# A new order of work, with one copy and half of a load given to ScalarE and five filler transposes taken out

## The chip, the cores and the metric

The kernel runs on one core of a Trainium2 chip. The metric is the device time of one execution in microseconds (us), lower is better. TensorE (PE) multiplies, VectorE (DVE), ScalarE (ACT) and GpSimd (POOL) do the elementwise work, and SyncE (SP) issues most of the transfers between the chip's memory and the on-chip memory. Each engine takes its own instructions strictly in the order in which they were written, and waits where a tile that it needs is not ready.

## The reference, cut to what matters

One transformer block over 16 batches (B) of 256 rows (S) of 256 features (E), all in float32:

```
a  = attention(x; 16 heads of 16, one key mask for all batches) @ Wo.T
a  = rms_norm(a) * (1 + gain(cond)) + shift(cond)        # per batch
kx, vx, rx = three mixes of a with a shifted by one row
k, v, r    = kx @ ak.T, vx @ av.T, rx @ ar.T
y  = sigmoid(r) * wkv(k, v)          # a decaying sum along the rows: two scans and a division
x1 = x + y @ ao.T
z  = fixed quaternion rotation of x1
g, u = fp4(z) @ fp4(w_gate).T, fp4(z) @ fp4(w_up).T       # 704 hidden features
out  = x1 + fp4(silu(g) * u) @ fp4(w_down).T
```

`fp4` rounds each block of 16 numbers to a 4-bit grid scaled by the block's maximum. The products above, 16 times, are nearly all of TensorE's work.

## The kernel before, in words

All work is cut into stages, each written as a Python generator that emits some instructions and yields. A stage has one letter and, for most, a batch number in hexadecimal: `a` (ask: load the next x, turn x, make q, k, v), `t` (attend), `l` (leave: Wo and the norm), `m` (mix: the recurrence), `r` (rotate), `h` and `i` (the hidden layer of the two row halves), `d` and `e` (turning its result), `f` (the down product and the output). The setup has stages too: `L` (loads), `Q`, `O`, `A` (turning the weights of the attention and the recurrence), `K` (mask and small vectors), `M` (gain and shift), `T`, `R` (decay and rotation), `W0` to `W5` and `V0`, `V1` (quantizing and turning the weights of the hidden layer) and `C` (a check at the end).

The string `ORDER`, 1884 tokens long, is the whole schedule: a loop takes its tokens one by one and resumes the named stage once. What a resumed stage emits is appended to the instruction stream of each engine in that order, so the string fixes the order on TensorE, VectorE, ScalarE, GpSimd and on SP's queue alike. Work that is emitted ahead of the loop (fillers of zero, the first activation, the first products on zeros) is merged in by the framework.

The string `BANKS` has one digit for each use of the eight PSUM banks, in the order of allocation. A product that is given a bank waits for the last reader of what was there before. A score group of `t` (lines 763 and 771) takes four banks at once, and the exponentials that empty them (L781) run on ScalarE, one for each bank. For batches 0 and 1, called whole, q and k are copied once by ScalarE (L726 and L737); later batches take a way through memory (`parts`, `spread`).

The opening: `load_x(0)` (L165) issues x of batch 0 in four transfers of 32 partitions each; Wq is issued by ScalarE's queue (L237), Wk and Wv by SP (L243). `turn_w` (from L325) turns each with four transposes into a bank (L334); after those of Wq, TensorE also transposes a tile of zeros eight times into a bank that nobody reads (L338). VectorE copies the turned Wq, Wk, Wv and Wo out of their banks (L342), ScalarE the four matrices of the recurrence (L344). VectorE turns x (L670), and the products of q and k (L632) and v (L644) follow. The fourth yield of `loads` issues ten small vectors from ScalarE's queue (L255 and L257), whose transpose is L350. x has two buffers, so the load of batch b + 2 waits until x of batch b has been turned.

Of the kernel before, what the change touches and what calls it, by code (L numbers as in the profile page):

```python
# [28 lines left out]
L af L Q L W1 a0 Q L Q a0 Q V0 a0 a1 a0 a0 a1 L W1 a0 W5 Q V0 L Q W1 a1 a1 a1 t0 a1 t0 K t0 W1 K W4 a0 t1 L W5 L  # L29
t1 a2 L t1 a2 W5 K W1 t0 W4 K W0 W4 K t0 R V0 a2 a3 M K A a3 a0 t0 L a1 W4 W5 a1 a2 M t0 K A t1 R t1 L t0 t0 t1  # L30
t0 W2 R O t0 t1 t0 W5 M T O W2 t1 t0 t0 a2 t1 V0 t0 a4 t1 L t1 t1 t0 t1 W3 t0 M t0 a2 W4 t1 W1 a2 t1 R V0 A l0
a2 R l0 a2 M W0 l0 V0 W0 W3 l0 W5 M A t1 W3 A t1 l0 W2 t1 T a3 R l0 l0 a2 m0 l0 a3 l1 A l1 W0 m0 m0 R W1 m0 m0
m0 m0 m0 a2 l1 a2 m0 l1 t2 W5 V0 R t2 t2 t2 a3 m0 V1 m0 m0 t2 t2 m0 W3 l1 t2 W3 m0 l1 m0 t2 t2 t2 t2 R t2 t2 t2
R m0 V0 t2 W0 W0 l1 m1 a3 W4 a3 a3 m0 V0 W3 l1 t2 m1 W3 a3 t2 t2 W2 W2 W0 A m1 m1 l2 A m1 m1 W4 l2 r0 m1 l2 m1
l2 r0 a4 a3 m1 m1 l2 l2 m1 m1 l2 m2 m1 m1 l2 m1 a3 m2 t3 a3 t3 m2 t3 t3 t3 m1 a4 t3 r0 r0 t3 r0 t3 a4 t3 t3 t3
m2 a4 t3 t3 a5 m2 W2 a4 V1 m2 t3 a4 t3 r0 t3 m2 m1 r0 t3 r0 a4 r1 m2 m2 a4 r1 t3 r1 r0 a4 W2 a5 a4 l3 l3 a6 m2
l3 V1 r1 m2 r0 a5 i0 a5 m2 i0 r1 r1 m2 i0 l3 V1 a4 t4 r1 m2 t4 t4 h0 i0 V1 t4 t4 i0 V1 m2 a5 t4 i0 h0 i0 h0 h0
t4 t4 i0 V1 t4 t4 t4 t4 i0 t4 a5 l3 t4 a5 r1 l3 r1 t4 m2 m2 h0 l3 a5 m3 l3 m3 t4 V1 a5 m3 i0 i0 a5 r2 r1 t4 h0
t4 m3 m3 r2 i0 m3 h0 a5 m3 l4 l4 a6 m3 l4 m3 m3 i0 a6 a5 l4 m3 m3 V1 a6 m3 t5 m3 t5 i1 i0 m3 t5 t5 i0 m3 t5 t5
e0 h0 i1 i1 e0 a6 t5 i1 t5 t5 t5 t5 h0 t5 t5 m3 i1 l4 t5 r2 a6 r2 t5 r2 l4 a7 t5 l4 i1 i1 d0 h0 i1 a6 h0 m4 r3  # L40
l4 m4 m4 h0 a6 a6 t5 d0 h1 m4 h0 r3 r2 i1 t5 h1 h1 a6 a6 i1 h1 m4 m4 h0 a7 r2 h1 i0 i1 h0 a6 h1 m4 a7 m4 a7 i1
m4 t6 h1 e0 t6 m4 m4 e0 t6 m4 l5 t6 i1 l5 t6 t6 r2 h0 d0 l5 m4 i1 h1 i1 t6 r2 m4 a7 m4 t6 d0 t6 l5 l5 t6 t6 r3
t6 t6 r3 t6 l5 a7 r2 e1 l5 r3 m4 a7 t6 d1 r3 i2 a7 r3 a7 f0 i1 i2 h2 i2 r3 i2 r3 f0 m5 l5 h2 e1 m4 a7 m5 a8 i2
h2 m5 h2 a7 i2 i2 h2 h1 r4 h2 h1 a7 h2 h1 d1 f0 h1 t7 i2 f0 t6 t7 f0 r4 t7 t7 h1 e1 t7 h1 m5 t7 t6 e1 t7 m5 h1
a8 t6 t7 m5 t7 t7 t7 a8 r4 h1 m5 t7 h2 d1 a8 r4 t7 d1 m5 r4 a8 a8 d2 l6 t7 m5 l6 l6 l6 i2 m5 i2 i2 r4 r3 m5 a8
i2 m5 r4 a8 l6 m5 h2 t7 a8 m5 h2 i2 h2 a8 m5 f1 l6 i2 m5 i2 i3 a9 a8 h2 h2 l6 i3 f0 f1 i3 h2 f1 i3 a8 l6 h2 m6
h2 d2 m6 m6 t8 f1 t8 t8 t7 t8 e2 i2 f1 i3 m5 t8 d2 r5 i3 i3 d2 r5 t7 a9 t7 t8 t8 t8 e2 t8 i3 e2 t8 a9 t8 a9 t8
t8 e3 m6 l7 m6 t8 l7 m6 t8 a9 r4 h3 h3 l7 l7 a9 r4 m6 m6 a9 l7 h3 e2 m6 a9 h3 l7 h3 a9 m6 m6 h3 f2 l7 i3 a9 i3
m6 i3 m6 h3 f2 i3 l7 m7 h3 m6 i3 i3 m6 m6 a9 aa m7 h3 i3 h3 h3 f1 h3 f2 m7 a9 e3 t9 t8 t9 t9 t9 f2 m6 r4 d3 f2
i3 t9 r6 h3 h3 t9 d3 e3 t8 h3 r6 t8 t9 h3 aa t9 t9 d3 e3 r5 r5 t9 r5 aa i4 i4 t9 l8 d3 t9 i4 m7 i4 aa i4 ab r5  # L50
h4 l8 i4 r5 m7 l8 h4 i4 f2 l8 aa t9 h4 h4 aa t9 m7 r5 h4 h4 l8 l8 i4 m7 h4 l8 t9 m7 m7 aa aa h4 m7 m7 i4 m7 m7
d4 m8 i4 i4 f3 aa aa l8 m7 m8 h4 m7 i4 i4 f3 m7 h4 m7 i4 m8 aa d4 r7 f3 h4 aa h4 i4 h4 ta f3 ta ta t9 f3 ta r7
ab h4 ac h4 ta e4 r7 t9 ab r7 e4 ta ab i4 ta r7 h4 r5 t9 ta ta r7 m8 ta ta ta ta r7 d4 r5 r6 ab r6 ta m8 m8 e4
m8 ab ab ta r6 m8 m8 m8 m8 l9 ab r6 h5 l9 m8 i5 h5 r6 i5 d4 m8 ab h5 l9 i5 h5 ab i5 e4 h5 i5 h5 h5 h5 ab l9 i5
m8 m8 r6 h5 h5 h5 tb h5 tb ta tb i5 tb m8 m8 r6 ab h5 l9 f4 tb l9 tb tb h5 i5 h5 tb e5 f4 ta ta e5 tb h5 tb tb
tb l9 f4 d5 r8 f4 f4 l9 tb r8 d5 r6 d5 ac m9 f4 tb r7 r8 r7 la tb la h6 h6 la r8 r8 h6 i5 i5 h6 m9 la d5 h6 la
i5 r7 i5 m9 m9 la ac m9 r8 m9 i5 m9 m9 ac i5 m9 la m9 ma m9 ac i6 m9 i7 m9 ac r8 h6 r8 ac m9 i5 i5 m9 i6 i6 ac
e5 m9 ac i7 h6 ac la i7 h6 ma e5 i6 f5 i7 f5 i6 i7 ma i6 i7 m9 f5 ad i6 f5 d6 h7 r9 h6 i6 i7 h6 h6 h6 ac f5 h7
h7 ac d6 tc tc r9 h6 tb h6 h7 tc ad tc ad ae h7 tc tc h6 tb h7 tc ad h7 tc tc tb r9 tc ad tc tc i7 ma h7 tc r9
h6 d6 ad i6 r9 ma tc e6 ma ad tc i6 i6 ma i6 h7 r9 r9 i7 f5 ma i6 r8 ma ad e6 r8 i6 lb ad h7 i7 h7 i6 h8 ma i6  # L60
i7 ma ad i7 ma e6 ma h7 h8 d6 i7 lb ad r9 e6 i7 h8 ma h7 ma r9 lb h7 i7 h8 td lb tc h7 ad td h8 td td td ma h8
lb h8 td e7 lb lb f6 lb f6 e7 mb td f6 i7 mb tc mb h8 ma tc h7 td td d7 f6 ra d7 i8 td f6 td i8 td ra r9 td e7
ae i8 i8 td d7 ra i8 mb i8 e7 f6 ra i8 i9 ae d7 i9 mb ra mb i9 i9 lc ra mb ae mb td h8 mb lc ae h8 i9 lc i8 i9
lc ra ae i9 lc mb h8 ae lc h8 mb h9 lc ra h8 mc ae h8 h9 h9 ra ae mb h9 ae h8 mb mb td d8 lc i8 h9 i8 mb h9 mc
# [1197 lines left out]
```

## Time and profile before

| What | us |
|---|---|
| median of 3 runs | 645.22 (645.11 to 645.31) |
| profiled execution, its own time | 645.53 |
| span of its instructions | 643.7 |
| TensorE busy | 635.6 (99%) |
| VectorE busy | 579.0 (90%) |
| ScalarE busy | 391.2 (61%) |
| GpSimd busy | 161.4 (25%) |

A line of the timeline has the start in us from the first instruction, the duration, the engine, the source line, the operation, the tiles (out<-in), the form and how many instructions are merged into it; what is in brackets is the idle time of the engine ahead of it and who ended it. PEld is TensorE's loading of weights, which overlaps the products. SPq and ACTq are the issuing of transfers by SP and ScalarE. A line of the waits names who waited for whom, with the total in us, the number of times and the longest. The end of a matmul is modelled, so its busy time can hide a wait; the distance from one start to the next does not. The granted clock of TensorE was 1.00 over the span.

| stretch of the span, us | PE busy | DVE busy | ACT busy |
|---|---|---|---|
| 0 to 40 | 38.86 | 34.16 | 25.98 |
| 40 to 200 | 159.65 | 142.37 | 116.41 |
| 200 to 400 | 199.95 | 178.77 | 125.40 |
| 400 to 600 | 199.49 | 190.51 | 107.51 |
| 600 to 643 | 37.67 | 33.14 | 15.88 |

### The profile page before, as it was taken

The page shows a single profiled execution, that of the slowest core. Times are in us where ns is not written, and L with a number is a line of the kernel's source. Part 1 is how long each engine was busy: PE and PEld are TensorE (multiplying, and loading weights), DVE is VectorE, ACT ScalarE, POOL GpSimd, SP SyncE. Part 2 cuts the span into 40 slices and gives each one's busy share as a digit, 9 for nine tenths or more (in the row PEclk, how much of TensorE's full clock was granted, in tenths as well). Part 3 has the DMA queues.
Part 4 walks back from the last instruction along what each step waited for, and adds up shares of the span by engine and source line. Part 5 has one row for each costly group of instructions (what it writes and reads, how often), then busy time and mean ns, then how long its engine had stood idle before and what let it go on. Part 6 is the DMA issues. An engine that isn't in the chain of part 4 may idle for free.

```text
span 643.7 us, 11304 instructions
## 1 busy us (share of the span) xinstructions
PE 635.6 (99%) x3936; PEld 475.9 (74%) x3936; DVE 579.0 (90%) x1178; ACT 391.2 (61%) x903; POOL 161.4 (25%) x214
## 2 busy tenths in 40 slices
PE   9999999999999999999999999999999999999996
PEld 7568877677777778777777777777877778776675
DVE  7897899889898877999998999999999999999994
ACT  3879784776757577674766546666483755433332
POOL 3353213222231122131221313113130122112220
PEclk9999999999999999999999999999999999999999
DMA  6643525334251425333420334203204100001001
GB/s 169 172 149 120 167 87 174 99 99 133 82 166 35 154 57 166 78 100 116 148 67 18 126 102 149 67 17 131 82 34 151 47 2 16 1 1 35 0 26 46
DMA packets 62848, 57.72 MB, mean 90 GB/s; under 512 B 36912, under 2 KB 40896, under 8 KB 62784
## 3 DMA queue, kind: packets, MB, share of 16 engines
q1 hardware_dynamic: 62416, 56.65, 29.4%
q8 instruction: 33, 0.54, 0.4%
q10 hardware_dynamic: 368, 0.28, 0.1%
q14 instruction: 31, 0.25, 0.1%
HBM read 38.03 MB, written 18.87 MB: 88 GB/s over the span
## 4 chain that ended last, share of the span: by engine, by line
PE 83%; DVE 12%; issue 2%; ACT 1%; DVEq 0%; ACTq 0%
PE ps L632 24%; PE ps L1003 18%; PE ps L793 9%; PE ps L644 8%; PE ps L1072 7%; PE pss L771 5%; PE ps L608 3%; PE ps L965 2%; PE pss L763 2%; DVE v L562 1%; DVE ps L554 1%; PE ps L656 1%; DVE ps L561 1%; DVE ps L1019 1%; PE ps L1079 1%
## 5 line engine op out<-in xcount | busy, mean ns | idle before, releaser
L1003 PE MATMUL ps<-guT,xqT 128*128 128x320 f32 (+1 forms) x512 | 165.6, 461 | 0.6 <-DVE v L562 0.6
L781 ACT ACTIVATE w<-pss 128x512 f32<-128x512 f32 x256 | 133.6, 609 | 32.7 <-PE pss L771 28.8
L1003 PEld LDWEIGHTS ps<-guT,xqT 128*128 128x128 f32 x512 | 94.7, 190 | 42.0 <-DVE v L562 1.7
L564 POOL TENSOR_TENSOR hq<-v,am 128x320 f32<-128x320 f32 (+1 forms) x64 | 50.0, 787 | 175.8 <-DVE v L562 154.4
L698 POOL TENSOR_TENSOR two<-two 128x512 f32<-128x512 f32 x28 | 35.7, 1275 | 114.2 <-ACT two L691 79.1
L793 PE MATMUL ps<-w,v_one 128*32 128x256 f32 x1024 | 63.1, 382 | 0.1
L559 ACT ACTIVATE m<-ps 128x384 bf16<-128x384 f32 (+1 forms) x64 | 29.8, 467 | 53.2 <-DVE ps L557 52.9
L1072 PE MATMUL ps<-hT,downT 128*128 128x256 f32 x260 | 59.6, 379 | 0.0
L1072 PEld LDWEIGHTS ps<-hT,downT 128*128 128x128 f32 x260 | 48.8, 190 | 8.1 <-ACT w L781 0.3
L936 DVE RECIPROCAL den<-den 128x512 f32<-128x512 f32 x16 | 53.5, 3343 | 0.1
L793 PEld LDWEIGHTS ps<-w,v_one 128*32 128x32 f32 x1024 | 31.8, 109 | 25.3 <-ACT w L781 3.6
L1015 ACT ACTIVATE th<-ps 128x320 f32<-128x320 f32 (+1 forms) x64 | 29.8, 469 | 26.9 <-PE ps L1003 26.1
L771 PEld LDWEIGHTS pss<-qT,kT 64*128 64x128 f32 x448 | 31.0, 185 | 19.3 <-issue 8.9
L771 PE MATMUL pss<-qT,kT 64*128 64x256 f32 x448 | 42.6, 306 | 0.1
L561 DVE SCALAR_TENSOR_TENSOR ps<-m,ps 128x384 f32<-128x384 bf16 (+1 forms) x64 | 33.2, 518 | 6.0 <-ACT m L559 5.8
L562 DVE SCALAR_TENSOR_TENSOR v<-m,ps 128x384 f32<-128x384 bf16 (+1 forms) x64 | 33.3, 521 | 4.9
L557 DVE SCALAR_TENSOR_TENSOR ps<-ps,rs 128x320 f32<-128x320 f32 (+1 forms) x64 | 34.1, 533 | 2.2
L554 DVE TENSOR_REDUCE ps<-ps 128x20 f32<-128x320 f32 (+1 forms) x64 | 34.1, 532 | 2.2
L608 PE MATMUL ps<-ident,hq 128*128 128x128 f32 (+1 forms) x204 | 34.5, 283 | 0.4 <-POOL hq L564 0.2
L1019 DVE SCALAR_TENSOR_TENSOR ps<-th,ps 128x320 f32<-128x320 f32 (+1 forms) x64 | 33.2, 518 | 1.1 <-PE ps L1003 0.4
L1017 DVE SCALAR_TENSOR_TENSOR th<-th,ps 128x320 f32<-128x320 f32 (+1 forms) x64 | 32.1, 507 | 0.4 <-ACT th L1015 0.3
L608 PEld LDWEIGHTS ps<-ident,hq 128*128 128x128 f32 (+1 forms) x204 | 22.0, 136 | 13.1 <-issue 4.0
(200 smaller groups left out, 1288.2 us busy)
## 6 DMA issues: line engine op xcount, KB each, us to landing
kept<-two SPq DMA_DIRECT2D x28, 512.0 KB, 3.2
qT<-kept SPq DMA_DIRECT2D x112, 128.0 KB, 2.9
kT<-kept SPq DMA_DIRECT2D x112, 128.0 KB, 2.8
x_sb<-in_x_dram SPq DMA_DIRECT2D x64, 64.0 KB, 2.3
out_dram<-o_sb SPq DMA_DIRECT2D x52, 64.0 KB, 1.9
out_dram<-o_sb SPq DMA_DIRECT2D x6, 128.0 KB, 2.3
raw<-in_L_ffn_w_down_dram SPq DMA_DIRECT2D x2, 352.0 KB, 3.9
raw<-in_L_ffn_w_gate_dram SPq DMA_DIRECT2D x5, 128.0 KB, 3.3
```

Of the source, the lines that this page charges most:

```text
L554: nc.vector.tensor_reduce(top, blk(x), AX.X, ALU.max, apply_absolute_value=True)
L562: nc.vector.scalar_tensor_tensor(v, m, BASE, x, ALU.max, ALU.subtract)
L564: nc.gpsimd.tensor_tensor(blk(dst), blk(v), bc(am), ALU.mult)
L608: nc.tensor.transpose(pt[0:n, (k - k0) * P : (k - k0 + 1) * P], src[:, k * P : k * P + n], ident)
L632: nc.tensor.matmul(pool_tile[:, ot * n : (ot + 1) * n], w[:, ct, ot * P : (ot + 1) * P], src[ct], start=(ct == 0), stop=(ct == E2 - 1),)
L644: nc.tensor.matmul(pool_tile[:, tt * E : (tt + 1) * E], srcT[:, ct, tt * P : (tt + 1) * P], w[:, ct, :], start=(ct == 0), stop=(ct == E2 - 1),
L771: nc.tensor.matmul(quad[2 * s + r][:, i * S : (i + 1) * S], kT[rows_, 2 * r + i, g, ks], qT[rows_, 2 * r + i, g, :], start=True, stop=True,)
L781: nc.scalar.activation(w[kt][:, r].rearrange("p i q -> p (i q)"), quad[r], AF.Exp)
L793: nc.tensor.matmul(pu[32 * r : 32 * r + 32, i * S : (i + 1) * S], vo[:, kt, 8 * g + 2 * r + i, :], w[kt][:, r, i, :], start=(kt == 0), sto ...
L936: nc.vector.reciprocal(flat(den), flat(den))
L1003: nc.tensor.matmul(p_[:, 0:n], xqT[:, ct, tt * P : (tt + 1) * P], guT[:, ct, base : base + n], start=(ct == 0), stop=(ct == E2 - 1),)
L1072: nc.tensor.matmul(pdn[:, 0:S], downT[:, k, h * P : (h + 1) * P], hT[:, k, :], start=(k == 0), stop=False)
```

## The change

`ORDER` is written anew, with the same tokens in the same numbers, and with it `BANKS`, which is again 749 digits long. In the opening, `L` (x0) and the turning of Wq come before everything else; the ten small loads come after the copy of k of batch 0 instead of after its qT; t0's and t1's score groups are placed differently; the loads of later weight blocks and x move on SP's queue. Three edits go with it: the last two of the four transfers of x0 are issued by ScalarE; the transposes of zeros after Wq are three instead of eight; and Wq's copy (`wt_q`) is done by ScalarE's copy at L344 and no longer by VectorE's at L342.

```diff
 ORDER = """
-L af L Q L W1 a0 Q L Q a0 Q V0 a0 a1 a0 a0 a1 L W1 a0 W5 Q V0 L Q W1 a1 a1 a1 t0 a1 t0 K t0 W1 K W4 a0 t1 L W5 L
-t1 a2 L t1 a2 W5 K W1 t0 W4 K W0 W4 K t0 R V0 a2 a3 M K A a3 a0 t0 L a1 W4 W5 a1 a2 M t0 K A t1 R t1 L t0 t0 t1
...
+L L Q Q L Q W1 L a0 a0 W5 a1 a0 Q a0 W1 Q a1 W1 W1 V0 W1 Q a0 W5 a0 a1 L a1 t0 V0 L W1 a1 K W5 a2 a0 a1 t0 L K
+t1 t0 K K V0 W2 a2 t1 a2 R R W5 t1 t0 L K K R K L a0 V0 t0 W2 A a1 W5 t0 A R a3 t1 W4 T W3 t0 a2 a1 L W1 t1 W4
...
 BANKS = """
-0123456702 1345670521 3470521364 7320516473 0275164237 5164023571 6043175415 3752406175 2406137541 6035741604
...
+0123456701 2346575601 2356012756 0123745620 7134562074 1635207416 2345712674 5162473016 2473501643 7504163750
...
@@ load_x
             for a in range(4):
-                queue[0].dma_start(
+
+                engine = nc.scalar if b == 0 and a > 1 and queue[0] is nc.sync else queue[0]
+                engine.dma_start(
@@ turn_w
             if name == "q":
                 busy = ps()
-                for i in range(8):
+                for i in range(3):
                     nc.tensor.transpose(busy[:, 0:P], blank, ident)
             yield
             wT[name] = wts.tile([P, E2, E], F32, tag="wt_" + name, name="wt_" + name)
-            if name in ("q", "k", "v", "o"):
+            if name in ("k", "v", "o"):
                 nc.vector.tensor_copy(flat(wT[name]), pt)
             else:
                 nc.scalar.copy(flat(wT[name]), pt)
```

## The prediction

> **What bounds the kernel now.** I read the page first: the busy line, the slices and the chain.
>
> ```profile
> PE 635.6 (99%) x3936; PEld 475.9 (74%) x3936; DVE 579.0 (90%) x1178; ACT 391.2 (61%) x903; POOL 161.4 (25%) x214
> PE   9999999999999999999999999999999999999996
> PE 83%; DVE 12%; issue 2%; ACT 1%; DVEq 0%; ACTq 0%
> ```
>
> TensorE is the bound, and it has almost nothing to lose: its slices are full from the first to the last but one. A busy matmul may still be a waiting one, so I went to the timeline for spacings. Eight passes over 256 columns follow each other in 1.73 us (L632, L644), four of 384 or 320 columns in 1.29 or 1.08 (L1003), 32 of L793 in 1.86, eight of L771 in 0.67, ten of L1072 in 2.16. Giving every TensorE step of the written order its spacing, the sum is 612.7 us. The first weight transpose starts at 4.07 and the last product ends at 638.86, so 22.1 us are not products. The product of m0 with a_k (L632) starts at 50.66 with 43.0 us of products before it: 3.6 us are lost in the opening, 18.5 after it. Those 18.5 are mostly seams, not waits: a group of L771 starts some 0.09 us late after another kind of product, L608 after L1079 some 0.28. The median of each kind of seam times its count gives 15.3 us; two or three microseconds of real waiting are left in 590. So the change can only earn much in the opening. Its timeline:
>
> ```profile
> 0.72 1.88 SPq L165 DMA_DIRECT2D x_sb<-in_x_dram  x4
> 1.24 1.28 ACT L199 ACT_TABLE_LOAD   x1 [1.24 <-PEq L1248]
> 2.73 2.74 DVE L295 TENSOR_SCALAR parq<-par 128x2 f32<-128x2 f32 x1
> 4.07 1.10 PE L334 MATMUL ps<-ident,ek 128*128 128x128 f32 x4
> 4.96 1.34 PE L338 MATMUL ps<-ident,blank 128*128 128x128 f32 x8
> 5.21 0.69 DVE L342 COPY wt_q<-ps 128x512 f32<-128x512 f32 x1
> 5.81 0.70 DVE L670 STREAM_TRANSPOSE xT<-x_sb 128x512 f32<-128x512 f32 x1
> 6.14 0.64 PE L334 MATMUL ps<-ident,xqT 128*128 128x128 f32 x4
> 6.62 1.95 PE L632 MATMUL ps<-xT,wt_q 128*128 128x256 f32 x8
> ...
> 8.66 0.52 ACTq L255 DMA_DIRECT2D rows<-in_L_cond_rms_scale_dram  x1
> ...
> 11.97 0.70 ACTq L257 DMA_DIRECT2D rows<-_cond_spectral_gate_dram  x1
> 12.72 0.59 ACT L737 COPY kT<-ps 128x512 f32<-128x512 f32 x1 [2.85 <-PE ps L632]
> ```
>
> VectorE copies the turned Wq and then turns x, one after the other; only then can the first real product start, at 6.62. From 8.66 to 12.67 ScalarE's queue issues ten small loads, and the copy of k behind them comes at 12.72 although its product was over at 10.3. The waits between 4 and 41 us say who holds TensorE afterwards:
>
> ```profile
> ACT w L781 <- PE pss L763: 3.6, 4, 1.1
> PEld pss L763 <- ACT w L781: 2.3, 4, 0.7
> PEld ps L793 <- ACT w L781: 1.3, 3, 0.8
> PEld ps L360 <- ACT w L781: 0.8, 1, 0.8
> PEld ps L350 <- issue: 0.8, 1, 0.8
> PEld ps L334 <- ACT w L781: 0.8, 1, 0.8
> ```
>
> TensorE and ScalarE wait for each other by turns: in batches 0 and 1 a score group (L763, four banks) needs banks that the exponentials (L781, four in 2.07 us) have not emptied.
>
> **The change, part by part.**
>
> *Five transposes of zeros fewer.* Eight took 4.96 to 6.14. 0.213 n + 0.109 (8 - n) = 1.18 gives n = 3: three at the slow spacing of everything before them (four in 0.89 at 4.07), five at the fast one. The five fast ones go: 5 x 0.109 = 0.55 us, and the turn of Wk starts at 5.59 if it has landed. The page "TensorE: Matmul & The Clock Gate" of the Trainium skill (What's actually happening) speaks against taking filler out: the array runs at half clock until it has been busy for about 3.4 us, and the window is free-running. By the row the step to the fast spacing comes near 5.5, and TensorE's work up to 5.59 is unchanged, so I count -0.55. By the rule the step could come a window later in some executions; the turn of Wk (0.48) and the first product (1.73) would then take twice as long, +2.2 instead. Three runs within 0.2 us of each other speak for the row.
>
> *The copy of Wq on ScalarE.* 0.69 us on VectorE become about 0.60 on ScalarE (the row of L344: 582 to 606 ns), which is idle from 2.73 to 8.60; it runs 5.21 to 5.81, hidden beside the turn of Wk (5.59 to 6.07). VectorE can turn x at about 5.2 (parq, 2.74 us long, still stands before it), done at 5.9. The first product could start at 6.07, 0.55 earlier.
>
> *Half of x0 issued by ScalarE.* SP saves two issues of 0.47 us, so Wk, the first gate weights, Wv and x1 are issued 0.94 earlier. Key Constraints in "Trainium Kernel Development and Optimization" says that all queues share the same 16 engines and a second one saves only issue time: by that, x0 lands at best 0.94 earlier, never at twice the rate. In the trace x0 was not what xT waited for (it started when the copy ended), so even this is worth only what the copy's move uncovers. On ScalarE the two issues take 0.94 us, either before the table load (1.20 to 2.14) or behind it and the activation at 2.53 (2.7 to 3.7). Landing took 2.3 to 3.4 us (x_sb's tile view). In the first case x0 is there before 5.2; in the second at 5.5 to 6.6, xT is done at 6.2 to 7.3, and all of the 0.55 may be lost, or 0.6 more. The trace cannot decide it: -0.55 to +0.6. The activation stands earlier in the code and needs only a tiny memset, so I lean to the late case and take -0.2.
>
> *The new order in the opening.* Walking TensorE, VectorE and ScalarE through the new order with the durations above, from a first product at 6.1: q 7.8, turn of Wv 8.3, k 10.0, q of batch 1 11.8. ScalarE now has the ten loads behind the copy of k, 10.3 to 14.3; queued behind them are the two qT copies of batch 1 (1.26) and its kT (0.59), and for these wait the exponentials, which start at 16.6 instead of 15.34. The rows land at about 15.8 (2.1 us after their issue), so their transpose (L350) holds TensorE 0.7 us with the v product queued behind it. On the other side, score groups stand back to back in two places instead of three (before: t1 after t0, t0's third after t1's second, t1's third after t0's fourth; each cost 0.8 to 0.9), and ScalarE's 4.05 us of idle time between 15.34 and 40.35 (1.05, 0.49, 0.68, 1.06, 0.77) are mostly closed because TensorE is ahead of it: the last exponential of batch 1 ends at 39.4 instead of 40.35. I reach m0's a_k product at 49.75, against 50.66: -0.9 with the -0.55 in it, so the rearrangement itself is worth -0.4. A second count: handoffs whose other-engine work is longer than the TensorE work put between. Up to 60 us of products, they were short by 9.0 us together and are now short by 5.5. The 9.0 became 3.6 us of loss; 5.5 at that rate make 2.2, a gain of 1.4. I take the middle, -0.9.
>
> *SP's queue.* x3, Wo, the third gate-and-up block and others change places; the third and fourth blocks wait for a raw buffer (until about 19 and 26 us), with av, ar and ao behind the latter. ao and ar are turned after 43 us, av at 40; landing takes 3. Hidden; without that cover 1 us each.
>
> *The order after the opening.* The same products, no engine newly short. VectorE (190.5 of 200 us busy from 400 to 600) has the same sum at the same places within 2 us, and the last twelve TensorE steps are the same. Short handoffs from 60 to 560 us of products: 9.8 us before, 10.6 now. Seams by the same medians: 15.3 before, 17.0 now, 0.8 of it from one pair seen once. Between nothing and +1.7 I take +0.5, as most of the added ones are of the 0.09 kind. The banks come with the order; their short reuses are in the counts.
>
> **The sum.** -0.2 (start) - 0.9 (opening) + 0.5 (later) = -0.6 us. The profiled execution took 645.53 us around its span of 643.7; it becomes 644.9, and the median of the runs, 0.31 below the profiled one, 645.22 - 0.6 = 644.6.
>
> **Rivals.** *The opening closes up* (faster): with x0 early (-0.55) and 2.2 of the 3.6 us gone, and no more seams, -2.75: 642.5. For it: TensorE would be ahead of ScalarE all the way. Against: ScalarE then needs every one of its 20-odd microseconds of work without a gap, and VectorE stands 1.5 us behind where t0's division frees a bank.
>
> *The ten loads decide* (slower): the exponentials of batch 0 start 1.25 us later, and ScalarE keeps its 4.05 us of gaps because the banks, not TensorE's lead, set them. Then everything up to 41 us is 1.25 late, with +0.5 of seams: 647.0. It turns to a loss from 2.8 us of remaining gaps on. Against it: only two back-to-back groups are left.
>
> *The moves do nothing*: x0 comes late, the copy waits beside it, and the order only exchanges waits: 645.2 plus 0.5, 645.7. The late half speaks for it, the shorter handoffs against.
>
> **How the numbers follow.** Within 0.2% (1.3 us, about what a measurement of this kernel can tell from no change) lie the sum, chance 0.38, and the rival that the moves do nothing, 0.17. Faster by more, with the opening closed or half closed: 0.32. Slower by more, the ten loads or a late clock step: 0.13. Range 642.6 to 646.5: it holds the rivals on both sides except the ends of them. The likeliest case's own range is 643.9 to 645.4.
>
> **What would show it.** Right: the transposes of zeros x3 in 0.6 us, the first product of L632 at 6.1 (x0 early) or 6.6 and later (late), the copy of Wq on ScalarE at 5.2, the last row load issued near 13.7, exponentials from 16.6, a_k's product (mx,wt_ak) near 50, and the same 99% on TensorE. Wrong: slow spacing after 6 us; ScalarE idle before L781 for more than 3 us up to 41 us; new waits of TensorE for VectorE or GpSimd past 60 us; a last product more than 1.3 us earlier or later than 638.86.

## The result, and the profile after

The kernel after the change takes 649.70 us (median of 4 runs, 648.10 to 650.24), the kernel before beside it 645.26 (645.11 to 645.35). The ratio is 1.0065, 95% interval 1.0046 to 1.0084: slower. The forecast was 644.6 with a range to 646.5; it has the wrong sign and the range does not hold the result. A second set of runs on another chip, with its own runs of the kernel before, gave 648.64 against 645.79, ratio 1.0046 (1.0030 to 1.0063). The profiled execution of after took 648.1 us around a span of 646.3.

The page of the kernel after: busy line, TensorE's slices, chain.

```profile
PE 635.7 (98%) x3931; PEld 476.7 (74%) x3931; DVE 574.2 (89%) x1177; ACT 392.3 (61%) x904; POOL 163.0 (25%) x214
PE   9899999999999999999999999999999999999996
PE 83%; DVE 9%; ACT 3%; DMA 2%; issue 1%; POOL 0%; SPq 0%; ACTq 0%; DVEq 0%; POOLq 0%
```

The page hardly differs from before: one slice of TensorE, the second, is an 8, and that is all it says on where 2.6 us went. The timeline says more. The kernel after, lines chosen from the opening (start, duration, engine, line, operation, tiles; in brackets the idle time before it and who ended it):

```profile
0.72 0.89 SPq L167 DMA_DIRECT2D x_sb<-in_x_dram  x2
1.31 0.91 ACTq L167 DMA_DIRECT2D x_sb<-in_x_dram  x2
4.93 0.84 PE L340 MATMUL ps<-ident,blank 128*128 128x128 f32 x3
5.17 0.59 ACT L346 COPY wt_q<-ps 128x512 f32<-128x512 f32 x1 [2.44 <-PE ps L336]
5.93 0.95 PE L336 MATMUL ps<-ident,xqT 128*128 128x128 f32 x4 [0.16 <-DMA xqT<-in_L_cond_Wk_dram]
6.20 0.71 DVE L672 STREAM_TRANSPOSE xT<-x_sb 128x512 f32<-128x512 f32 x1 [5.22 <-DMA x_sb<-in_x_dram]
7.06 1.97 PE L634 MATMUL ps<-xT,wt_q 128*128 128x256 f32 x8 [0.18 <-DVE xT L672]
...
11.32 0.49 ACTq L257 DMA_DIRECT2D rows<-in_L_cond_rms_scale_dram  x1
12.62 0.35 SPq L616 DMA_DIRECT2D raw<-in_L_ffn_w_down_dram  x1
14.41 0.70 ACTq L259 DMA_DIRECT2D rows<-_cond_spectral_gate_dram  x1
15.16 1.27 ACT L728 ACTIVATE qT<-ps,parq 128x512 f32<-128x512 f32 x2 [3.32 <-DMA rows<-in_L_attn_mix_k_dram]
16.91 0.22 PE L352 MATMUL ps<-ident,rows 37*128 37x37 f32 x1 [0.48 <-DMA x_sb<-in_x_dram]
17.09 2.08 ACT L783 ACTIVATE w<-pss 128x512 f32<-128x512 f32 x4
```

The Wq copy runs on ScalarE at 5.17 as planned, but VectorE still does not turn x before 6.20: now it waits for x0 itself (5.22 us, ended by the transfer). Wk's turn starts at 5.93, when Wk has landed; the three transposes of zeros are over before, and TensorE stands idle for it. The first real product comes at 7.06, 0.44 later than before. The ten row loads go out between 11.3 and 15.1, and everything of ScalarE behind them follows: the qT copies at 15.16, the exponentials at 17.09 (before 15.34). (The trace names a load of x as the end of the wait at 16.91; the transpose itself reads only the rows.) Somewhat later, on TensorE:

```profile
22.37 1.14 PE L765 MATMUL pss<-qT,kT 32*128 32x512 f32 x8
24.86 0.63 PE L336 MATMUL ps<-ident,den 128*128 128x128 f32 x4 [1.35 <-DMA den<-in_L_attn_Wk_dram]
```

The turn of a_k waits 1.35 us for its load, a wait that before does not have. The kernel before, the load of w_down, the first exponentials, the load of a_k and its turn:

```profile
6.94 0.35 SPq L614 DMA_DIRECT2D raw<-in_L_ffn_w_down_dram  x1
...
15.34 2.09 ACT L781 ACTIVATE w<-pss 128x512 f32<-128x512 f32 x4
...
17.60 0.45 SPq L243 DMA_DIRECT2D den<-in_L_attn_Wk_dram  x1
...
22.84 0.60 PE L334 MATMUL ps<-ident,den 128*128 128x128 f32 x4
```

The waits of after between 4 and 41 us (who for whom, total, times, longest), and then one of SP's queue over the whole span:

```profile
ACT qT L728 <- DMA rows<-in_L_attn_mix_k_dram: 3.3, 1, 3.3
ACT w L783 <- PE ps L795: 3.3, 3, 1.3
...
DVE am L536 <- DMA raw<-in_L_ffn_w_down_dram: 1.4, 1, 1.4
PE ps L336 <- DMA den<-in_L_attn_Wk_dram: 1.4, 1, 1.4
ACT w L783 <- PE pss L765: 0.9, 2, 0.6
PEld pss L765 <- ACT w L783: 0.9, 3, 0.3
```

```profile
SPq L616 <- DMA rows<-in_L_cond_rms_scale_dram: 3.0, 1, 3.0
```

Why a load on SP's queue waits for one on ScalarE's can be read from the trace's record of each issue, which names the semaphore (a counter that other instructions wait for) that its landing raises. SP and ScalarE use the same eight by turns, and an issue waits until the transfer that had its semaphore before has landed. In after, w_down has that of the first row load, which ScalarE issues at 11.32; neither its data nor its buffer needs that load.

TensorE and ScalarE wait for each other at the scores much less than before (0.9 and 0.9 us, before 3.6 and 2.3): that part of the new order does what the prediction had it do. In its place stand waits for transfers, and 3.3 us of ScalarE behind value products (L795) that come later.

To place the loss I use the sum of the prediction: for a TensorE step, its start, minus the 4.05 at which the first weight transpose starts, minus the spacings of all steps ahead of it in the written order. What is left is time in which TensorE did no step at its usual pace ("lost"). The five missing transposes make the sum of spacings 0.55 shorter after, so the same lost time is a step 0.55 earlier.

| lost before this step, us | before | after | after with 8 zeros |
|---|---|---|---|
| first product, q of batch 0 | 0.32 | 1.31 | 0.86 |
| first scores of batch 0 | 0.47 | 1.47 | 1.02 |
| transpose of the rows | 0.51 | 2.41 | 2.31 |
| q of batch 2 | 1.48 | 2.61 | 2.51 |
| v of batch 1 | 1.48 | 4.18 | 2.69 |
| first value product of batch 1 | 2.42 | 5.03 | 4.65 |
| a_k product of m0 | 3.59 | 5.81 | 5.43 |
| a_r product of m0 | 4.02 | 6.97 | 6.58 |
| out product of r0 (74 to 77 us) | 4.88 | 8.14 | 7.75 |
| scores of t3 (81 to 85 us) | 4.98 | 8.23 | 7.84 |
| end of the last product | 22.13 | 25.46 | 24.94 |

From t3 to the end before loses 17.15, after 17.23. So nearly the whole loss of 3.33 (2.78 in time, with the 0.55) arises in the first 80 us, in five places: before the first product (+0.99), at the rows (+0.90), at the load of a_k (+1.57), between the a_k and a_r products of m0 (+0.73) and before r0 (+0.31). In between, 1.2 us are won back, where before has score groups back to back.

### The profile page after: what moved, and what is told of

Read it like the earlier page. It is cut to its first block, busy times and chain, and to the rows that moved or that the text cites. A ratio compares the mean times of both kernels' runs of the same rounds, so it can differ in the third digit from the quotient of the medians.

```text
span 646.3 us, 11312 instructions
## 1 busy us (share of the span) xinstructions
PE 635.7 (98%) x3931; PEld 476.7 (74%) x3931; DVE 574.2 (89%) x1177; ACT 392.3 (61%) x904; POOL 163.0 (25%) x214
## 4 chain that ended last, share of the span: by engine, by line
PE 83%; DVE 9%; ACT 3%; DMA 2%; issue 1%; POOL 0%; SPq 0%; ACTq 0%; DVEq 0%; POOLq 0%
PE ps L634 23%; PE ps L1005 19%; PE ps L795 9%; PE ps L1074 8%; PE ps L646 8%; PE pss L773 5%; PE ps L610 3%; PE ps L967 2%; DVE v L564 1%; PE ps L658 1%; DVE ps L556 1%; PE ps L1081 1%; PE pss L765 1%; DVE ps L559 1%; DVE ps L563 1%
## 5 line engine op out<-in xcount | busy, mean ns | idle before, releaser
L1005 PE MATMUL ps<-guT,xqT 128*128 128x384 f32 (+1 forms) x512 | 165.4, 461 | 0.2 <-DVE v L564 0.2
L795 PE MATMUL ps<-w,v_one 128*32 128x256 f32 x1024 | 63.2, 382 | 0.1
L561 ACT ACTIVATE m<-ps 128x320 bf16<-128x320 f32 (+1 forms) x64 | 29.8, 466 | 49.7 <-DVE ps L559 49.7
L795 PEld LDWEIGHTS ps<-w,v_one 128*32 128x32 f32 x1024 | 32.9, 109 | 25.9 <-ACT w L783 4.8
L1017 ACT ACTIVATE th<-ps 128x320 f32<-128x320 f32 (+1 forms) x64 | 29.6, 466 | 21.7 <-PE ps L1005 15.8
L564 DVE SCALAR_TENSOR_TENSOR v<-m,ps 128x320 f32<-128x320 bf16 (+1 forms) x64 | 33.4, 521 | 4.7
L941 POOL TENSOR_TENSOR yT<-num,den 128x512 f32<-128x512 f32 x16 | 20.4, 1274 | 55.4 <-DVE den L938 55.4
L563 DVE SCALAR_TENSOR_TENSOR ps<-m,ps 128x320 f32<-128x320 bf16 (+1 forms) x64 | 33.1, 517 | 1.3 <-ACT m L561 1.2
```

The source lines that it names most:

```text
L795: nc.tensor.matmul(pu[32 * r : 32 * r + 32, i * S : (i + 1) * S], vo[:, kt, 8 * g + 2 * r + i, :], w[kt][:, r, i, :], start=(kt == 0), sto ...
L1005: nc.tensor.matmul(p_[:, 0:n], xqT[:, ct, tt * P : (tt + 1) * P], guT[:, ct, base : base + n], start=(ct == 0), stop=(ct == E2 - 1),)
```

## The experiments

Four theories are named in the expectations. A: the queues of ScalarE and SP decide (the ten small row loads, and loads that wait behind others). B: the split of x0 decides. C: the order of TensorE's steps decides; in the first two groups this is looked for behind the opening, from the third on inside it. D: the step of TensorE's spacing from slow to fast, which filler was covering, comes late. Each group shares one chip and its runs of the kernel before.

### First group: edits and order apart

Before took 645.93 here, and its runs lay between 645.35 and 648.62, so these ratios are wider than the later ones. Wq landed late on this chip (its turn starts at 4.4 to 4.8 instead of 4.1).

The new ORDER and BANKS alone, with the old zeros, copy and loads (BANKS belongs to its ORDER; no run has the new one of the two without the other):

```diff
 # against the kernel before
-ORDER, BANKS: as before
+ORDER, BANKS: as after
```

> The new order and banks alone; the three small edits are undone (four transfers of x0 on SP, eight transposes of zeros, the copy of Wq on VectorE). Theory A (the ten small loads, issued behind the copy of k of batch 0, hold ScalarE's and SP's queues, so that the matrix a_k lands only near 25 us): that wait of TensorE, 1.3 us in the changed kernel, is still there, and the time is 648 or more. Theory B (the halved load of x0 makes x0 and Wk late): the first q product starts at 6.6 as before and the time falls to about 646. Theory C (the order after the opening is worse): 648 with the loss past 85 us.

Measured: 651.53, ratio 1.0080 (1.0052 to 1.0108). The order alone is slower, and the wait for a_k is there (1.39 us), as theory A had it. Lost at t3 11.22, at the end 28.43: 17.2 in between, as in before. So it is not the order behind the opening. In this execution Wk's turn starts at 7.32 and the slow spacing lasts to 10.3: 2.92 are lost before batch 0's k product, where before loses 0.38. So about half of these 5.2 us (0.8%) is the start of that execution and not the steps behind it.

The three edits in the old order:

```diff
 # against the kernel after
-ORDER, BANKS: as after
+ORDER, BANKS: as before
```

> The old order and banks with the three small edits. Theory A: the opening of the old order stays whole, so 645.2 plus or minus 0.7. Theory B: the first q product is late, near 7.0 instead of 6.62, and the time is 645.7 to 646.5. Theory C: 645.

Measured: 648.48, ratio 1.0026 (1.0014 to 1.0039). The edits without the order cost about 1.7 us by the ratio (0.9 to 2.5), and 2.55 by the medians: the runs of before on this chip lie in two clumps, near 645.7 and near 648.

The kernel after with x0 issued by SP alone:

```diff
-engine = nc.scalar if b == 0 and a > 1 and queue[0] is nc.sync else queue[0]
+engine = queue[0]
```

> The changed kernel with all four transfers of x0 back on SP, all else kept. Theory A: the first q product comes forward, to 6.1 to 6.5, but the loads still hold the queues: 647.5 to 649.5. Theory B: 645.5 to 646.5.

The kernel after with the row loads right behind batch 0's qT copies:

```diff
-... a0 W1 Q a1 W1 W1 V0 W1 Q a0 W5 a0 a1 L a1 t0 ...
+... a0 L W1 Q a1 W1 W1 V0 W1 Q a0 W5 a0 a1 a1 t0 ...
```

> The changed kernel with one token of the order moved: the ten small loads are issued behind qT of batch 0, as in the kernel before, instead of behind its kT. Theory A: the load of w_down no longer waits on SP for the small loads, a_k lands before it is needed, exponentials start 1 to 1.5 us earlier: 645 to 646.5. Theory B and C: no change from the changed kernel, 648 to 650.

Measured: 651.99 (ratio 1.0090, 1.0056 to 1.0124) and 651.48 (1.0076, 1.0047 to 1.0105). Both medians lie above after, with intervals that overlap its own, and both profiled executions have the slow spacing until 9.7 and 8.6, so neither says what its edit is worth. With three zeros the start itself is unsteady, which the next group takes up.

### Second group: the zeros

The kernel after once more; after with eight zeros; before with three.

> The changed kernel itself, to stand beside the next three on one chip, with a second trace of it. Theory A (queues: the transfers of SP and ScalarE share eight completion counters, so a transfer on one queue waits for an earlier one of the other) expects the same waits for the small loads and for a_k as in its first trace. Theory D[...] expects the step to the fast spacing at a different time from the first trace, 6.4 us, and the time to move with it.

```diff
-for i in range(3):   # after
+for i in range(8):
```

> The changed kernel with eight transposes of zeros instead of three. Theory A: the five fall into a wait for Wk and x0 that is there anyway, no change within 0.3 us. Theory D: the step to the fast spacing comes a window earlier in most executions, 0.7 to 1.7 us faster than the changed kernel and less spread between its runs.

```diff
-for i in range(8):   # before
+for i in range(3):
```

> The kernel before with three transposes of zeros instead of eight, all else as it was. Theory A: 0 to 0.55 us faster than before. Theory D: the step to the fast spacing comes later than 5.5 us, the q product of batch 0 runs slow, and the time is 1 to 2 us above the kernel before.

| kernel | median | ratio to before (645.79) |
|---|---|---|
| after, again | 648.64 | 1.0046 (1.0030 to 1.0063) |
| after, eight zeros | 648.44 | 1.0049 (1.0032 to 1.0065) |
| before, three zeros | 646.75 | 1.0016 (1.0008 to 1.0024) |

In the old order, taking out the five transposes costs 0.96 us instead of gaining 0.55. The kernel before with three zeros, TensorE:

```profile
4.95 0.84 PE L338 MATMUL ps<-ident,blank 128*128 128x128 f32 x3
6.37 1.14 PE L334 MATMUL ps<-ident,xqT 128*128 128x128 f32 x4 [0.58 <-DMA xqT<-in_L_cond_Wk_dram]
7.30 3.13 PE L632 MATMUL ps<-xT,wt_q 128*128 128x256 f32 x8
```

And the kernel after, run again:

```profile
6.50 1.13 PE L336 MATMUL ps<-ident,xqT 128*128 128x128 f32 x4 [0.61 <-DMA xqT<-in_L_cond_Wk_dram]
7.62 3.48 PE L634 MATMUL ps<-xT,wt_q 128*128 128x256 f32 x8
```

Wk is not there when the three zeros end; TensorE idles, the turn of Wk runs at the slow spacing (1.13 instead of 0.64), and eight products of q take 3.1 to 3.5 us instead of 1.95. In these two the slow spacing lasts until 9.8 and 10.7; in the profile of before it ended at 5.6. These were slower executions of their kernels (648.2 and 649.95), so the medians lose less. In the new order the zeros cannot be told from nothing (648.64 and 648.44): three or eight, its other losses are there. So after with eight zeros, which starts at the fast spacing at 6.5, is the better base for the order: +2.65 us, with the split and the copy in it. It differs from after in one thing more: its w_down has the semaphore of an earlier load of SP's own and goes out at 10.73 instead of 12.62 and 14.84, and its trace has no wait of TensorE for a_k. The time is the same.

The row loads directly behind the Wq copy, in after with three zeros:

```diff
-L a0 a0 W5 a1 a0 Q ... a1 L a1 t0
+L a0 a0 L W5 a1 a0 Q ... a1 a1 t0
```

> The changed kernel with one token of the order moved: the ten small loads are issued behind the copy of Wq, ahead of qT of batch 0, where ScalarE has nothing to do. Theory A: the load of w_down and what follows it on SP start 2 to 4 us earlier, a_k is there when it is turned (1.3 us of waiting gone), exponentials start by 16 us: 1.5 to 2.5 us faster than the changed kernel. Theory D: no gain, since the clock's step comes before that.

Measured: 649.65 (1.0070, 1.0053 to 1.0087). Rows early are no help: the slow spacing lasts until 9.8 here, and then ScalarE, which issued rows until 11.8, makes the Abs step of the first gate block late, so that TensorE waits for hq (1.5 us on PEld, 0.6 on PE) in front of the rows.

### Third group: x0, the row loads, single edits in the old order

Half of x0 on ScalarE, in the kernel before:

```diff
-queue[0].dma_start(
+engine = nc.scalar if b == 0 and a > 1 and queue[0] is nc.sync else queue[0]
+engine.dma_start(
```

> The kernel before with nothing changed but half of x0 on ScalarE's queue. Theory B (split makes x0 late and Wk no earlier in effect): xT starts after 5.81 (6.2 to 6.3), first product at 7.1 instead of 6.62, time +0.5: 646.3 beside 645.8. The rule that only issue time is saved: xT waits for the copy of Wq as before, first product 6.62, no change.

Measured: 646.26 against 645.62, ratio 1.0011 (1.0004 to 1.0018): the split alone costs 0.64. The kernel before with the split, VectorE:

```profile
5.20 0.69 DVE L343 COPY wt_q<-ps 128x512 f32<-128x512 f32 x1 [1.85 <-PE ps L335]
6.84 0.71 DVE L671 STREAM_TRANSPOSE xT<-x_sb 128x512 f32<-128x512 f32 x1 [0.94 <-DMA x_sb<-in_x_dram]
```

VectorE is done with Wq at 5.9 and then waits 0.94 for x0; the first product comes at 7.61. x0 is later with two queues than with one: in the three traces where VectorE is idle and x0 is on SP alone, xT starts at 5.57 to 5.86; in the twelve with the split, at 6.20 to 6.84. Two traces (the row loads on GpSimd, below) record every landing: with SP alone the four quarters of x0 land at 3.27, 4.20, 4.83 and 5.35 and Wk at 5.99; with the split at 3.05 and 4.27 (SP), 4.52 and 6.39 (ScalarE), and Wk, issued 0.98 earlier, at 6.20.

x0 back on SP in the new order, eight zeros:

> The new order and the ScalarE copy with eight zeros, x0 all on SP's queue: only the split of x0 is undone against the run with eight zeros (648.4). Theory B (the split makes x0 land later, first product 7.15 instead of 6.62): x0 lands by 5.8, the first product comes at 6.6 to 6.7, the time falls by 0.5 to 647.9. The rule that issue time is all that is saved: x0 lands up to 0.9 later, first product 7.6 or later, 648.9 to 649.3. Theory A: rows and w_down as late as before, so nothing of the later 2 us changes.

Measured: 649.53 (1.0067, 1.0052 to 1.0083) where the split gave 648.44 on another chip (1.0049). xT starts at 5.81, yet the first product only moves from 7.15 to 7.02, because the turn of Wk stands before it; and w_down is issued at 14.17 instead of 10.73, so that VectorE waits 3.4 us for it, and a_k is late again (0.6). Here a row load had w_down's semaphore before (2.6 us of SP's wait), so the two kernels differ in this too. In the new order the split is not the cause, and may be a help; the two ratios' intervals overlap.

The row loads on GpSimd's queue, new order and eight zeros, then in the kernel before:

```diff
-nc.scalar.dma_start(out=rows[at, :] ...
+nc.gpsimd.dma_start(out=rows[at, :] ...
```

> The new order with the three edits and eight zeros, and the ten small row loads issued on GpSimd's queue (idle from 6 to 14 us) instead of ScalarE's. Theory A (the ten issues stand in ScalarE's queue ahead of the second qT copies and kT, so the exponentials start 2.2 us later than before, and the row transpose holds TensorE 0.8 to 1.2 us): the 1.25 us between batch 0's first scores and the row transpose go, exponentials start by 16.0, and the time falls from 648.4 to 646.5 to 647.2. Theory C (the place of the turns of the gate blocks and of the second kT in the order decides): TensorE then waits for GpSimd's hq or for a bank instead, and the time stays within 0.5 of 648.4. Theory D (clock alone): no change.

> The kernel before with nothing changed but the ten small row loads on GpSimd's queue. Theory A: ScalarE's copy of k comes at 10.6 to 11.5 instead of 12.72, exponentials can start 0.5 to 1.2 us earlier, and up to 1 us of the opening goes: 644.8 to 645.5 beside 645.8. Rival: in the old order the row transpose at 15.2 sits right behind the scores and the banks set the pace; nothing changes (645.6 to 646.0). If an issue on GpSimd costs much more than 0.3 us, the rows land after 15.2 and it is slower, 646.5 or more.

Measured: 655.06 (1.0144, 1.0129 to 1.0160), and 645.85 against 645.62 (1.0003, 0.9995 to 1.0012). The first fell outside everything expected of it. The rows stand behind GpSimd's hq in the new order and are issued at 13.7 to 19.2; TensorE waits for them. The new order with the rows on GpSimd:

```profile
14.84 1.89 PE L634 MATMUL ps<-xT,wt_k 128*128 128x256 f32 x8
...
16.77 0.58 ACT L739 COPY kT<-ps 128x512 f32<-128x512 f32 x1 [1.79 <-PE ps L634]
17.25 2.07 ACT L783 ACTIVATE w<-pss 128x512 f32<-128x512 f32 x4
...
21.23 0.29 PE L352 MATMUL ps<-ident,rows 37*128 37x37 f32 x1 [4.50 <-DMA rows<-_cond_spectral_gate_dram]
21.45 3.78 PE L646 MATMUL ps<-wt_v,xT 128*128 128x256 f32 x8
```

Rows that come late are paid in full, and after 4.5 us of idle time the eight products behind their transpose take 3.78 us instead of 1.99. But look at ScalarE: with no row load in its queue the exponentials still start only at 17.25. The kT copy of batch 1, which stands ahead of them, waited 1.79 for its product (14.84), and the new order puts that product behind batch 0's scores. Theory A alone is not enough; a part of C is inside the opening.

### Fourth group: what the opening is made of

All three on the new order with eight zeros. Batch 1's k product ahead of batch 0's first scores (with its bank digits moved along):

```diff
-a0 a1 L a1 t0 V0 L W1 a1 K W5
+a0 a1 L a1 a1 t0 V0 L W1 K W5
```

> The new order with eight zeros, and one step moved: batch 1's k product stands ahead of batch 0's first scores again, as before. Theory C (the late k product holds the first exponentials): kT of batch 1 at 15.6 to 16.4 instead of 17.07, exponentials from 16.2 to 17.0, 647.4 to 648.0 beside 648.4. Theory A (the ten issues hold ScalarE until 15.56 and the rows until 17.2): qT still starts at 15.6, exponentials at 17.5, the row transpose still waits until 17.3, 648.2 to 648.6.

The row loads on SP's queue behind x2, and both together:

```diff
-nc.scalar.dma_start(out=rows[at, :] ...      # and: W5 a1 a0 Q ... a1 L a1
+nc.sync.dma_start(out=rows[at, :] ...        # and: W5 a1 L a0 Q ... a1 a1
```

> The new order with eight zeros, and the ten row loads on SP's queue behind x2 instead of on ScalarE's. Theory A: rows land by 15.9, the row transpose waits for nothing, ScalarE is free from 11.9; 647.2 to 647.8. Theory C: kT of batch 1 still waits for its product until 16.6, exponentials at 17.2, and TensorE waits for hq or a bank instead; 648.0 to 648.5. Rival to both: the ten issues (3 us) push x3, w_down and Wo back on SP's queue and VectorE waits for w_down in front of cols; 648.5 to 650.

> Both: batch 1's k product ahead of batch 0's first scores, and the ten row loads on SP's queue behind x2 (new order, eight zeros). If the late product and the loads together make the loss of the opening: exponentials from 15.3 to 15.8, row transpose at 16.3, lost time at batch 0's v product near 1.1 as at the first product, 646.2 to 647.0. If the loss comes from elsewhere (w_down late, x0 late): 647.5 or more.

| lost before this step, us | before | 8 zeros | k first | rows on SP | both | both, a_k ahead |
|---|---|---|---|---|---|---|
| first product | 0.32 | 0.86 | 0.98 | 1.07 | 1.31 | 1.12 |
| transpose of the rows | 0.51 | 2.31 | 1.93 | 1.61 | 1.85 | 1.66 |
| q of batch 2 | 1.48 | 2.51 | 2.13 | 2.15 | 2.09 | 2.13 |
| v of batch 1 | 1.48 | 2.69 | 2.31 | 4.38 | 4.09 | 2.32 |
| first value product of batch 1 | 2.42 | 4.65 | 4.27 | 5.31 | 5.19 | 5.82 |
| a_k product of m0 | 3.59 | 5.43 | 5.05 | 6.09 | 5.97 | 6.60 |
| end | 22.13 | 24.94 | 24.77 | 25.96 | 25.59 | 26.54 |
| median, us | 645.26 | 648.44 | 648.00 | 649.15 | 648.68 | 651.97 |
| ratio | | 1.0049 | 1.0041 | 1.0054 | 1.0045 | 1.0095 |

(Before here is the first profile; each ratio is to the runs of before beside it.) The k product first gives 0.4 at the rows and keeps it to m0; at the end 0.17 of it is left in the trace: 648.00. Against the 8-zero kernel this is within the intervals. The exponentials still start at 17.3, held by the row loads. With both moved the exponentials start at 16.30 (15.3 to 15.8 was expected) and the rows' extra loss is down to 0.5; and then the gain is gone at one place. The kernel with both, TensorE and SP's queue:

```profile
13.09 0.38 SPq L616 DMA_DIRECT2D raw<-in_L_ffn_w_down_dram  x1
...
18.79 0.95 SPq L590 DMA_DIRECT2D raw<-in_L_ffn_w_gate_dram  x2
...
21.04 1.71 SPq L245 DMA_DIRECT2D den<-in_L_attn_Wk_dram  x1
...
22.40 1.14 PE L765 MATMUL pss<-qT,kT 32*128 32x512 f32 x8
25.31 0.63 PE L336 MATMUL ps<-ident,den 128*128 128x128 f32 x4 [1.77 <-DMA den<-in_L_attn_Wk_dram]
```

The row loads made w_down late (13.09); VectorE waits for it (1.50 us before L536, at 16.26), so the raw buffer comes free late; the third gate-and-up block waits for that buffer at the head of SP's queue until 18.79; and a_k's load stands behind it. This is also the wait seen in the profile of after, where w_down is issued at 12.62, the block at 18.16 and a_k at 20.43.

The copy alone in the kernel before:

```diff
-if name in ("q", "k", "v", "o"):
+if name in ("k", "v", "o"):
```

> The kernel before with nothing changed but the copy of the turned Wq on ScalarE. x0 lands near 5.8, so xT starts where it started before (5.8) and the first product stays at 6.6: 645.4 to 645.9 beside 645.6. If x0 had landed by 5.2, xT would be done by 5.9 and the first product come at 6.6 all the same, as the turn of Wk ends then: no gain either. Slower by more than 0.4 would mean that the copy holds up something on ScalarE's queue that no row of before shows.

Measured: 645.93 against 645.72, ratio 1.0002 (0.9994 to 1.0010). No effect.

### Fifth group: the last wait, and more filler

The kernel with both moves, and the loads of Wc and a_k now ahead of the third gate-and-up block:

```diff
-t0 L K t1 t0 K K V0 W2 ... t0 L K K R K L a0
+t0 L L L K t1 t0 K K V0 W2 ... t0 K K R K a0
```

> The new order with eight zeros, batch 1's k product first, the ten row loads on SP's queue, and now also the loads of Wc and a_k ahead of the third gate-and-up block on that queue. If the late a_k is what remains in the opening: no wait of TensorE for a_k's load, lost time at batch 1's v product 2.3 instead of 4.1, time 646.4 to 647.2 beside 648.7 for the same without the two loads moved. If banks held by late exponentials take the gain back by batch 0's and 1's last score groups: 647.5 to 648.7.

Measured: 651.97 (1.0095, 1.0080 to 1.0111), slower than without. The wait for a_k is gone, as expected (lost at v of batch 1 2.32 instead of 4.09), and its profiled execution, at 649.55 the fastest of the four and 0.8 above that of the kernel without the two loads moved, shows what took its place. That kernel, TensorE and VectorE:

```profile
16.30 0.89 DVE L536 TENSOR_REDUCE am<-raw 128x44 f32<-128x704 f32 x1 [1.73 <-DMA raw<-in_L_ffn_w_down_dram]
...
31.64 0.72 DVE L805 STREAM_TRANSPOSE u<-ps 128x512 f32<-128x512 f32 x1
32.41 2.31 PE L765 MATMUL pss<-qT,kT 32*128 32x512 f32 x10 [1.63 <-DVE u L805]
```

VectorE lost 1.73 waiting for w_down and is behind until 31.6, when it frees a bank (31.01 without the two loads moved, 27.10 in before). A score group needs that bank, and TensorE waits. Why its other three runs took about 652 no trace shows; their granted clock is 0.995 beside 0.999 in the profiled one, and 0.4% of the span would be 2.6 us (an estimate), about the difference.

Twelve zeros in the kernel before:

> The kernel before with twelve transposes of zeros instead of eight, the other way from the change. Theory D (TensorE's idle time before the turn of Wk delays the clock's step): no idle time of TensorE between Wq and Wk and the step by 5.5 always; four more at 0.109 cost 0.44 where Wk has landed by then and nothing where it lands at 6.4. Together 645.4 to 646.0 beside 645.7, with a narrower spread. If the filler only costs: 646.1 to 646.3.

Measured: 645.72 against 645.70 (1.0004, 0.9995 to 1.0012), the spread no narrower. Eight are enough; more do no harm. None of the kernels beats the kernel before.

## Why the prediction was wrong, step by step

The step that failed is the start and the opening, -0.2 and -0.9 in the sum. The prediction had a_k's product of m0 at 49.75 instead of 50.66; it came at 52.34, 1.7 later than before and not 0.9 earlier, because in the new order TensorE or VectorE waits for Wk, x0 and a_k, which it took as landed or hidden, and because the rows come later than it had them. Nearly all of the other 1.1 of the 2.78 us comes between there and 85 us; for everything behind the opening the sum had +0.5. Part by part:

*Five transposes of zeros fewer, -0.55: wrong.* Measured alone in the old order, +0.96. The prediction weighed the row (the slow spacing ends near 5.5) against the clock-gate rule of the Trainium skill ("TensorE: Matmul & The Clock Gate", What's actually happening), and took the row. What failed is a condition that it named and dropped: "if it has landed". Wk's turn could start only at 5.93 to 6.52, TensorE had idle time before it, and the slow spacing lasted past 7 us in six of the seven profiles with three zeros. The rule's 2.2 is about what the profiled execution of before with three zeros shows (2.4 more than before lost by its k product), one of its slower ones; its median is less than half of that. "Three runs within 0.2 us" were runs with the filler in place and could not speak for a kernel without it.

*The copy of Wq, hidden: right.* It costs and gives nothing (1.0002). One reading under it did not hold: parq, 2.74 us long in before and taken to stand ahead of xT, runs behind xT in after, for 0.17 us at 7.31.

*Half of x0 on ScalarE, -0.2 within -0.55 to +0.6: wrong sign.* Alone +0.64. The prediction argued about when the two issues go out and leaned to the late case; they went out early, at 1.31, and x0 landed later all the same. The landing had been bounded from one side only: the rule in Key Constraints ("Trainium Kernel Development and Optimization"), that all queues share 16 engines, was read as "at best 0.94 earlier", where it also leaves room for Wk and the gate block, issued 0.98 earlier, to take their share while x0 is still on its way. That x0's last quarter lands later is shown; that this sharing is the reason is argued. The page "DMA: Bandwidth & Descriptors" (Queues, rings and completion order) has each engine take the queues in turn, a packet at a time, and each queue in its order, so that the half of x0 on ScalarE's queue also stands behind Wq there; no run separates the two.

*The opening, -0.9: wrong, and the largest term.* Of the 2.6 us between 49.75 and 52.34: the walk started from a first product at 6.1 and it was at 7.06: 1.0 of it. It had the exponentials at 16.6 (measured 17.09) and the rows at about 15.8 (their transpose 16.91), so the late rows were seen and undersized by half a microsecond to one. What it missed altogether is the a_k wait, 1.57. The second count, of short handoffs that "make 2.2 at that rate", treated handoffs as independent of when the data land; in the new order TensorE and ScalarE did wait less for each other, and other waits decided.

*SP's queue, "hidden; without that cover 1 us each": the cover was gone for one load.* The step checked av, ar and ao, which stand behind the fourth block, and not a_k behind the third. The block is held by a buffer, the buffer by VectorE, VectorE by w_down. Of the 5.7 us by which w_down is issued later (12.62, before 6.94), 3.0 are the wait for the row load whose semaphore it shares; most of the rest is its new place behind x2, whose last quarter is issued at 9.21. Where the trace names the wait for a_k, its price was 0.6 to 1.8, not 1.

*The order after the opening, +0.5: right in kind, too large.* From t3 to the end after loses 17.23, before 17.15, e1's order alone 17.21. But the bound between opening and rest was set too early: between 50 and 77 us another 1.0 is lost, at m0's second stretch (+0.73, where two score groups of batch 2 take 2.41 us instead of 1.69; the trace puts their waits to copies and exponentials on ScalarE) and before r0 (+0.31). No run takes these two apart.

*The rival "the ten loads decide", 647.0,* was the nearest: the exponentials came 1.75 late, it had 1.25, and ScalarE's queue behind the loads was as it said. It is not the cause by itself. Taking the loads off that queue lifts that wait and the time does not fall (649.15), since they then delay w_down. Three of the signs listed under "wrong" came: slow spacing after 6 us, ScalarE idle before the exponentials for more than 3 us up to 41 (4.2), and a last product more than 1.3 later (641.64 instead of 638.86).

The account of the whole, each part against its own runs of before: old order, zeros +0.96, split +0.64, copy +0.2 (not told from 0), 1.8 in sum; measured together 1.0026, which is 1.7 (2.55 by medians). New order with copy, split and eight zeros +2.65; with three zeros +2.85 on that chip; with copy and eight zeros but no split +3.9, on another chip and with w_down late. So in the old order the parts add within what this chip's runs can tell, and with the new order they do not.

What the runs settle is that the loss comes with the order (and its BANKS) and arises in the opening, and that no single wait makes it. The clearest sign is the kernel with eight zeros: w_down goes out early, TensorE does not wait for a_k, and it is no faster than after, because a score group then waits for a bank. The kernel after with eight zeros, TensorE and VectorE, and below it the kernel before:

```profile
29.70 3.86 PE L765 MATMUL pss<-qT,kT 32*128 32x512 f32 x16
30.47 0.72 DVE L805 STREAM_TRANSPOSE u<-ps 128x512 f32<-128x512 f32 x1
```

```profile
26.96 2.99 PE L763 MATMUL pss<-qT,kT 32*128 32x512 f32 x16
27.10 0.73 DVE L803 STREAM_TRANSPOSE u<-ps 128x512 f32<-128x512 f32 x1 [0.20 <-PE ps L793]
```

In before VectorE empties the bank as soon as the value product is over; in the new order it has no idle time ahead of u and comes 0.77 into the group, for which TensorE's queue of weight loads waits 0.9. From batch 1's v product to its first value product this kernel loses 1.96, before 0.94. The kernel with the k product first, where w_down goes out at 10.32, loses the same 1.96 there.

When w_down goes out is settled by the traces too. In after (both traces), in the kernel with the order alone and in the one with x0 back on SP, its semaphore was last used by a row load on ScalarE's queue, SP waits 2.6 to 5.1 us for that load, and w_down goes out at 12.6 to 16.2. With eight zeros and with the k product first it is a quarter of x2 on SP's own queue, with the rows on GpSimd one of x1, and w_down goes out at 10.3 to 10.7. Open stays what the same opening would give with w_down as early as before (6.94) and VectorE in time for the bank, and what the old opening would give with the new order behind it.

## What to carry to other kernels

Filler that looks idle may cover the landing of a load: before taking it out, ask when the next operand lands, not when the filler ends, and run the filler's removal alone. In an opening where loads are still landing, walk the transfers as carefully as the engines: for every load in a queue ask which buffer the entry ahead of it waits for, and who frees that buffer. A second issuing queue brings the issues forward together, and the load that is needed first can land later for it while the others land no earlier. Ask also which transfer had a load's completion semaphore before it: two queues that look independent can be tied there.

## What the runs showed of the hardware

*The step of the spacing goes with the filler and with idle time.* The spacing of TensorE's first products goes from 427 to 216 ns (256 columns) at a time that differs between executions. In the 13 profiled executions with eight or twelve zeros it came at 4.3 to 7.1 in twelve, and at 10.3 in the one where Wq and Wk landed latest; in the 7 with three zeros at 6.4, 7.2, 8.6, 9.7, 9.8, 9.8 and 10.7. While the spacing was slow, TensorE stood idle for at most 0.4 us in those twelve, for 0.7 in the thirteenth and for 0.2 to 0.9 in the seven, ahead of Wq or of Wk. That filler brings the step forward is shown (the time of the kernel before with three zeros, +0.96); that idle time alone sets it is not: at 0.9 it came at 7.2 once.

*After the step, a short idle time does no harm, a long one does.* In five executions that were fast by 5.0, TensorE stood idle for 0.3 to 0.7 us ahead of Wk and went on at the fast spacing. After 4.5 us without a product in the middle of the opening, eight products took 3.78 us instead of 1.99.

*The granted clock hardly shows it.* As a mean over the span it is 0.99 to 1.00 in all profiled executions; the one with the 4.5 us has the lowest, 0.993, but the one with the step at 10.7 has 1.000.

*An issue costs what its engine makes it.* A row load takes 0.23 to 0.73 us to issue on ScalarE or SP, 0.52 to 0.75 on GpSimd; the ten held GpSimd for 5.5 us and ScalarE for 3.8.
